# The last rows of each expert's list in one tile of its own size, with the odd quarter of 32 rows computed in column groups of TensorE

## The chip, the core and the metric

The program runs on one core of one Trainium2 chip. Its time is the device time of one execution, in microseconds; of several executions the median is given. A profile is one more execution, recorded by the hardware profiler. In it PE is TensorE (matmuls), PEld its weight loads, DVE is VectorE, ACT is ScalarE, POOL is GpSimd and SP the engine whose queue issues most of the DMA transfers.

## What is computed

One layer over 4096 nodes of 256 features: a graph attention with four heads over a dense 0/1 adjacency matrix, and then a mixture of eight experts of which each node uses two. Cut to what matters:

```python
def gnn(x, adj, W, a1, a2, Wr, br, gamma, beta):
    h = einsum('nd,hdk->hnk', x, W)
    e = leaky_relu(s_row[:, :, None] + s_col[:, None, :], 0.2)
    att = softmax(where(adj > 0, e, -9e15))
    y = elu(att @ h) + x @ Wr + br
    return layernorm(y) * gamma + beta

def ffn(x, Wg, bg, W1, b1, W2, b2):          # 8 experts, top 2
    top_w, top_i = top_k(x @ Wg + bg, 2)
    w_dense = sum(one_hot(top_i) * softmax(top_w)[..., None])
    for e in range(8):
        h = gelu(x @ W1[e] + b1[e])          # 256 -> 1024
        out += w_dense[:, e:e + 1] * (h @ W2[e] + b2[e])

x = x + gnn(layernorm(x), adj, ...)
x = x + ffn(layernorm(x), ...)
```

## The kernel before

**Attention.** The first part, to about 779 us, runs over four passes of 1024 columns. After each pass the 1024 nodes are finished (ELU, residual, layer norms) and routed: their normalised rows are scattered into one list for each expert, in HBM (`lists`, 4608 rows of room each), by indirect DMA from POOL. So the lists are known in steps, after 2048, 3072 and all 4096 nodes.

**Jobs of the experts.** The second part takes rows from the lists in jobs. A job is one expert and a tile of its list. Its rows are brought in, turned so that features lie on the partitions (`turn`), multiplied by W1 (`up`: for each of 8 blocks of 128 hidden features two matmuls into a PSUM tile `ph`, then a Gelu on ScalarE into `hT`), and multiplied by W2 (`down`: for each chunk of 128 rows eight matmuls into `po`). VectorE makes `o` from `po`, each row's share and the scaled second bias, and POOL adds `o` to the rows of the output by an indirect scatter-add. Every scatter-add waits until the one before it has landed. Scores, weights and rows are fp32.

There are 33 jobs. Nine full tiles of 256 rows are planned from the first 2048 nodes (`early`) and eight from 3072 (`mid`). What is left of each list is planned when all nodes are routed, in `plan_rest`: tiles of 256 rows (`rest`, of which 14 are always run), and tiles of 384 rows for lists whose last tile would hold 128 rows or fewer (`broad`, of which two are always run). The two `broad` jobs come right after the full tiles, then the 14 of `rest`. In rows of TensorE's work this is 17 x 256 + 2 x 384 + 14 x 256 = 8704, in 68 chunks. If the lists need more tiles than these, an optional part (`further`) runs them after everything else, behind a test of counters.

**Rooms.** Weights, rows, `xT` and `hT` have two buffers each, `ph` three PSUM banks, `po` two, `o` nine.

**Order.** TensorE's order is fixed by hand (`queue`, L458) until the last two blocks of nodes are routed; they are finished while the first five jobs run (`between`, L1835). After that the scheduler orders by the program's priorities, which gives `ph` of a job, the next tile's transposes, `po` of the job, and so on. SP issues transfers one after another in the order of the loop: for each job `fetch` (L1681) brings b2, w1 and w2, one job ahead; each waits in the queue until its buffer is free. The rows of full tiles come as whole rows (`load_full`, L1857) and are turned by TensorE. Tiles 1 to 15 are loaded ahead of the loop, into 15 buffers, and tile 16 in its third round. The rows of later jobs come as 32-column blocks (`load_blocks_of`, L495) and are turned by VectorE. Both loads wait for the scatters noted so far in `listed`:

```python
        def load_rows_of(t, i, xr):
            rows = t["parts"] * CH
            first = entry(t, 1, i, E * LIST - WT)
            ins = nc.sync.dma_start(
                xr, lists[bass.ds(first, rows), :].rearrange("(c p) d -> p c d", p=CH)
            ).ins
            for i in listed:
                after(ins, i, "rows of the tile")
```

`listed` is emptied when the experts begin (the earlier scatters are long done), and filled again by the routing of the last two blocks: eight scatters each, noted in the fourth and in the fifth round of the loop. After the second block `plan_rest` fills the tables, and POOL writes zeros behind the end of each list (L443), so that a tile may read past it.

Of the kernel before, what the change touches and what calls it, by code (L numbers as in the profile page):

```python
# [18 lines left out]
P = 128  # L19
# [10 lines left out]
CH = P  # L30
TT = 2 * CH
WT = 3 * CH
# [11 lines left out]
def gat_then_moe(  # L44
# [35 lines left out]
    LATE = (2 * N + E * (TT - 1)) // TT - BOTH  # L80
    SURE, SURE_WIDE = 14, 2
# [52 lines left out]
    inside = numbers("inside", [CH, 3], [[CH, 3]], step=1)  # L134
# [82 lines left out]
    def forward(apart, stack):  # L217
# [49 lines left out]
        def tables(tag, width):  # L267

            return {
                "expert": moe_tile(f"expert{tag}", [P, width]),  # L270
                "mark": moe_tile(f"mark{tag}", [P, width]),
                "own": moe_tile(f"own{tag}", [P, width, E]),
                "place": moe_tile(f"place{tag}", [P, width]),
                "rows": moe_tile(f"rows{tag}", [P, width]),
                "float": moe_tile(f"float{tag}", [P, 2, width]),
                "int": moe_tile(f"int{tag}", [P, 2, width], I32),
                "past": moe_tile(f"past{tag}", [P, width, E]),
                "parts": 3 if tag == "w" else 2,
                "upto": moe_tile(f"upto{tag}", [P, E]),
            }  # L280
# [61 lines left out]
        early, mid, rest, broad = tables("e", EARLY), {}, {}, {}  # L342
# [32 lines left out]

        def plan_rest():
# [3 lines left out]
            broad.update(tables("w", E))  # L380
# [7 lines left out]
            tiles = whole("r", left, 0.0)  # L388
            full = whole("h", left, float(CH))
            odd = moe_tile("odd", [P, E])  # L390
            nc.vector.tensor_tensor(odd, tiles, full, OP.subtract)
            nc.vector.tensor_scalar(full, tiles, 2.0, None, op0=OP.is_ge)
            nc.vector.tensor_tensor(odd, odd, full, OP.mult)
            nc.vector.scalar_tensor_tensor(tiles, odd, -2.0, tiles, op0=OP.mult, op1=OP.add)
            plan(rest, LATE, n, tiles, used)
            nc.vector.tensor_tensor(used, used, tiles, OP.add)
            plan(broad, E, n, odd, used)
            counts = moe_tile("counts", [P, 4])
            nc.vector.tensor_copy(counts[:, 0:1], rest["upto"][:, E - 1 :])
            nc.vector.tensor_copy(counts[:, 1:2], broad["upto"][:, E - 1 :])  # L400
            more = moe_tile("more", [P, 3])
            nc.vector.tensor_scalar(more[:, 0:1], counts[:, 0:1], SURE + 0.5, None, op0=OP.is_gt)
            nc.vector.tensor_scalar(
                more[:, 1:2], counts[:, 1:2], SURE_WIDE + 0.5, None, op0=OP.is_gt
            )
            nc.vector.tensor_copy(more[:, 2:3], strayed)
            nc.vector.tensor_reduce(counts[:, 2:3], more, AX.X, OP.max)
            nc.vector.tensor_copy(counts[:, 3:4], strayed)
# [3 lines left out]
            for t, name in (rest, "r"), (broad, "w"):  # L412
                width = t["own"].shape[1]
                spare = moe_tile(f"spare{name}", [CH, width, t["parts"]])
# [71 lines left out]
        def load_rows_of(t, i, xr):  # L486
            rows = t["parts"] * CH
            first = entry(t, 1, i, E * LIST - WT)
            ins = nc.sync.dma_start(
                xr, lists[bass.ds(first, rows), :].rearrange("(c p) d -> p c d", p=CH)  # L490
            ).ins
            for i in listed:
                after(ins, i, "rows of the tile")

        def load_blocks_of(t, i, xb, known):  # L495


            first = entry(t, 1, i, E * LIST - WT)
            rows = lists[bass.ds(first, t["parts"] * CH), :]
            begun = [nc.sync.dma_start(known, rows[:, D:].rearrange("(c p) d -> p c d", p=CH))]  # L500
            for c in range(DC):
                for a in range(P // Q):
                    here = c * P + a * Q
                    begun.append(nc.sync.dma_start(
                        xb[ts(a, Q), c], rows[:, here : here + Q].rearrange("(k p) d -> p k d", p=Q)
                    ))
            for ins in begun:
                for i in listed:
                    after(ins.ins, i, "rows of the tile")
# [1163 lines left out]
        count = kept.tile([P, 4], I32, name="count")  # L1673
# [5 lines left out]
        full_rows = [xr0]  # L1679

        def fetch(t, i):  # L1681

            nch = t["parts"]
# [3 lines left out]
            else:  # L1687
                xr = work.tile([P, DC, t["parts"] * CH // Q, Q], F32, tag="xr", name="xr")
                known = work.tile([CH, t["parts"], RW - D], F32, tag="known", name="known")
# [11 lines left out]
            job = {"t": t, "i": i, "xr": xr, "known": known, "w1": w1, "w2": w2, "nch": nch, "b2b": b2b}  # L1701
            job["last"] = t is rest and i == SURE - 1
# [4 lines left out]
        def prepare(job):  # L1707
# [17 lines left out]
            else:  # L1725
                no = work.tile([CH, nch], F32, tag="no", name="no")
                nc.vector.scalar_tensor_tensor(
                    no, inside[:, :nch], t["rows"][:CH, i : i + 1], t["spare"][:, i, :],
# [15 lines left out]
        def turn(job):  # L1744
            xr, nch = job["xr"], job["nch"]
# [7 lines left out]
            xT = work.tile([P, DC, nch * CH], F32, tag="xT", name="xT")  # L1753
# [10 lines left out]
        def up(job, xT):  # L1764

            nch = job["nch"]
            hT = work.tile([P, FC, nch * CH], F32, tag="hT", name="hT")
            for f in range(FC):
                tag = ("acc00", "acc10", "acc01")[turns[0] % 3]
                ph = ps.tile([P, nch * CH], F32, tag=tag, name="ph")  # L1770
# [15 lines left out]
        def down(job, hT):  # L1786
# [4 lines left out]
            for k in range(nch):  # L1791
                b2s.append(work.tile([CH, D], F32, tag="b2s", name="b2s", bufs=4 if apart else 3))
# [3 lines left out]
            for k in range(nch):  # L1796
                if optional[0]:
                    po = bank([CH, D], "po")
                else:
                    po = ps.tile([CH, D], F32, tag=("acc11", "den")[rounds[0] % 2], name="po")  # L1800
                rounds[0] += 1
                for f in range(FC):
                    order_of(nc.tensor.matmul(  # L1803
                        po, hT[:, f, ts(k, CH)], w2[:, f, :], start=(f == 0), stop=(f == FC - 1)
                    ))
                if k + 1 == nch:
                    yield
# [3 lines left out]
                else:  # L1811
                    o = work.tile([CH, D], F32, tag="o", name="o", bufs=2 * LAG - 3 if apart else 2)
                given_out.append(nc.vector.scalar_tensor_tensor(  # L1813
                    o, po, share[:, k : k + 1], b2s[k], op0=OP.mult, op1=OP.add
# [3 lines left out]
                    bass.IndirectOffsetOnAxis(ap=ids[:, k : k + 1], axis=0), o, None,  # L1818
# [4 lines left out]
                else:  # L1823
                    add()  # L1824

# [24 lines left out]
        todo += [(broad, i) for i in range(SURE_WIDE)] + [(rest, i) for i in range(SURE)]  # L1850
# [6 lines left out]
        def load_full(i):  # L1857
            xr = work.tile([CH, 2, RW], F32, tag="early", name="early", bufs=BOTH - 2)
# [3 lines left out]
        for i in range(1, BOTH - 1):  # L1862
# [7 lines left out]
        for i in range(len(todo)):  # L1870
# [3 lines left out]
            if i == 2:  # L1874
                load_full(BOTH - 1)
# [23 lines left out]
        def further():  # L1899
# [3 lines left out]
            with (  # L1903
# [3 lines left out]
                for k, t, least, top in (0, rest, SURE, LATE), (1, broad, SURE_WIDE, E):  # L1907
                    tiles = held(k, top)
                    with ExitStack() as nest:
                        for i in range(least, top):  # L1910
                            nest.enter_context(tc.If(tiles > i))
                            given_out.clear()
                            job = fetch(t, i)
                            for _ in down(job, up(job, turn(job))):
                                pass
# [5 lines left out]
    with tc.If(held(2, 1) > 0):  # L1921
        further()
        with tc.If(held(3, 1) > 0):
            with ExitStack() as again:
                held, further, rest_of_sums, _ = forward(False, again)
                with tc.If(held(2, 1) > 0):
                    further()
# [35 lines left out]
```

## Time and profile before

| | |
|---|---|
| median of 3 runs | 1286.02 us (1284.5 to 1286.14) |
| the profiled execution, its own time | 1281.97 us |
| its span in the profile | 1280.3 us |
| TensorE busy | 1260.4 us, 98% of the span |
| VectorE busy | 848.7 us, 66% |
| ScalarE busy | 466.8 us, 36% |
| POOL busy | 241.2 us, 19% |
| `w` from HBM, 66 transfers | 1024 KB each |
| chain that ended last | TensorE 92%, VectorE 4% |

The span runs from the first to the last recorded instruction; the execution's own time holds also what lies around it. Busy time of TensorE says that something was in its pipeline, not that it ran at its peak. A matmul of fp32 appears as two instructions, its two passes. In a group, the mean is the latency of one instruction; instructions overlap, so what one costs is the distance between the starts of consecutive ones. The words after an arrow name what ended the idle time ahead of an instruction.

### The profile page before, as it was taken

To read this page: it belongs to the slowest core of one execution; us is meant where nothing else is said; L and a number is where in the kernel's file an instruction comes from. 1 tells how busy PE (TensorE), PEld (TensorE's weight loads), DVE (VectorE), ACT (ScalarE), POOL (GpSimd) and SP (SyncE) were. 2 spreads that over 40 slices of the span, in tenths; PEclk is the share of its full clock that TensorE was granted. 3 is DMA by queue.
4 is the path that set the end of the run, shared out by engine and by line. 5 is a ranking of instruction groups with operands and counts; after the bars stand their busy time and mean duration, and the time that the engine had idled before them with its cause. 6 is when DMAs were issued, how large, how long until landed. Compare 5 with 4: busy or idle time off the path is not lost.

```text
span 1280.3 us, 23272 instructions
## 1 busy us (share of the span) xinstructions
PE 1260.4 (98%) x9102; PEld 698.4 (55%) x9102; DVE 848.7 (66%) x1619; ACT 466.8 (36%) x977; POOL 241.2 (19%) x217
## 2 busy tenths in 40 slices
PE   9999999999999999999999999999999999999997
PEld 5444444332233322322334326878888877888886
DVE  6998887979999999999999995834111111211110
ACT  4322322265432464323644314432333333233232
POOL 4000000001004400006010051244222222122122
PEclk9999999999999999999999999999999999999999
DMA  6334433527433647335563326966866776888882
GB/s 211 114 118 129 152 100 100 189 82 170 154 104 122 206 115 212 103 104 164 128 198 128 120 75 221 284 179 207 260 162 175 198 180 140 201 216 186 209 207 30
DMA packets 144152, 203.36 MB, mean 159 GB/s; under 512 B 49785, under 2 KB 113265, under 8 KB 143649
## 3 DMA queue, kind: packets, MB, share of 16 engines
q1 hardware_dynamic: 122128, 159.16, 41.4%
q0 software_dynamic: 20416, 36.07, 12.8%
q10 hardware_dynamic: 1488, 6.55, 1.4%
q8 instruction: 73, 1.20, 0.4%
q14 instruction: 47, 0.38, 0.1%
HBM read 169.53 MB, written 29.07 MB: 155 GB/s over the span
## 4 chain that ended last, share of the span: by engine, by line
PE 92%; DVE 4%; issue 1%; another core or an unknown queue 1%; DMA 1%; ACT 1%; POOLq 0%; SPq 0%; DVEq 0%; ACTq 0%
PE acc L1112 33%; PE po L1803 18%; PE ph L1773 18%; PE den L1121 16%; PE pr L967 2%; DVE w L1602 2%; PE ph L1015 2%; PE pt L521 1%; PE acc L808 1%; PE ptx L1167 0%; DMA early<-lists 0%; PE pt L694 0%; PE ptr L1405 0%; PE pl L1178 0%
## 5 line engine op out<-in xcount | busy, mean ns | idle before, releaser
L1112 PE MATMUL acc<-w,ha 128*32 128x512 f32 x4096 | 669.9, 593 | 1.3 <-ACT u L1315 0.9
L1602 DVE SCALAR_TENSOR_TENSOR w<-er,eb,am 128x1024 f32<-128x1024 f32 x496 | 606.1, 1275 | 30.4 <-PE den L1121 30.1
L1121 PE MATMUL den<-w,unit 128*2 128x512 f32 x2048 | 466.9, 592 | 0.1
L1112 PEld LDWEIGHTS acc<-w,ha 128*32 128x32 f32 x4096 | 184.5, 110 | 292.8 <-issue 253.8
L1519 ACT ACTIVATE am<-adj 128x1024 bf16<-128x1024 int32 x124 | 130.6, 1054 | 346.4 <-DVE w L1602 208.3
L1773 PE MATMUL ph<-xT,w 128*128 128x256 f32 (+1 forms) x1056 | 243.1, 388 | 3.8 <-issue 3.1
L1803 PE MATMUL po<-w,hT 128*128 128x256 f32 x1088 | 240.2, 379 | 0.0
L1777 ACT ACTIVATE hT<-ph,bias 128x256 f32<-128x256 f32 (+1 forms) x264 | 126.4, 481 | 299.0 <-PE ph L1773 199.9
L1773 PEld LDWEIGHTS ph<-xT,w 128*128 128x128 f32 x1056 | 201.1, 191 | 40.3 <-issue 5.2
L1803 PEld LDWEIGHTS po<-w,hT 128*128 128x128 f32 x1088 | 205.5, 190 | 27.7
L1813 DVE SCALAR_TENSOR_TENSOR o<-po,share,b2s 128x256 f32<-128x256 f32 x66 | 31.9, 483 | 258.9 <-PE po L1803 237.1
L1121 PEld LDWEIGHTS den<-w,unit 128*2 128x2 f32 x2048 | 93.5, 85 | 148.2 <-issue 139.8
L1824 POOL DMA_INDIRECT out<-o,ids x66 | 103.4, 1566 | 338.6 <-DMA out<-o,ids 213.5
L1299 POOL DMA_INDIRECT lists<-xe,at x64 | 88.3, 1380 | 266.6 <-issue 184.3
L525 DVE COPY xT<-pt 128x256 f32<-128x256 f32 x12 | 5.1, 424 | 61.9 <-PE pt L521 61.9
L1795 ACT ACTIVATE b2s<-b2b,share 128x256 f32<-128x256 f32 x68 | 30.8, 503 | 0.0
L967 PE MATMUL pr<-wr,xT 128*128 128x256 f32 x128 | 30.4, 381 | 0.2 <-ACT er L1061 0.2
L1355 POOL DMA_DIRECT2D xf<-in_x x6 | 8.1, 1346 | 103.7 <-ACT xf L1354 103.7
L1035 POOL DMA_DIRECT2D residual<-rb x6 | 4.7, 785 | 121.2 <-DVE rb L982 121.2
L967 PEld LDWEIGHTS pr<-wr,xT 128*128 128x128 f32 x128 | 24.1, 190 | 5.4 <-issue 0.9
L1015 PE MATMUL ph<-wall,xT 128*128 128x264 f32 x96 | 24.6, 399 | 0.0
L1015 PEld LDWEIGHTS ph<-wall,xT 128*128 128x128 f32 x96 | 17.2, 189 | 12.6 <-issue 10.2
(396 smaller groups left out, 653.8 us busy)
## 6 DMA issues: line engine op xcount, KB each, us to landing
w<-in_L_ffn_W SPq DMA_DIRECT2D x66, 1024.0 KB
adj<-in_adj SPq DMA_DIRECT2D x126, 512.0 KB
er<-parts ACTq DMA_DIRECT2D x3, 2048.0 KB
b2b<-in_L_ffn_b SPq DMA_DIRECT2D x33, 128.0 KB
early<-lists SPq DMA_DIRECT2D x16, 260.0 KB
residual<-rb POOLq DMA_DIRECT2D x8, 512.0 KB
rb<-residual SPq DMA_DIRECT2D x8, 512.0 KB
out<-y POOLq DMA_DIRECT2D x8, 512.0 KB
```

Of the source, the lines that this page charges most:

```text
L967: order_of(nc.tensor.matmul(pr[:, k, :], turned[b][:, c, ts(t0 + k, P)], wr[:, c, :], start=(c == 0), stop=(c == DC - 1),))
L1015: order_of(nc.tensor.matmul(phs[t - t0], xT[:, c, ts(t, P)], wall[:, c, :], start=(c == 0), stop=(c == DC - 1),))
L1112: queue(nc.tensor.matmul(acc[half][h // 2][here : here + Q, :], ha[:, j, h * K + g * Q : h * K + (g + 1) * Q], w[half][h], start=(j == 0), ...
L1121: queue(nc.tensor.matmul(den[here : here + HB, :], unit[:, j, h, 1 - half : 1 - half + HB], w[half][h], start=(j == 0 and half == 0), stop ...
L1299: ins = nc.gpsimd.indirect_dma_start(lists, bass.IndirectOffsetOnAxis(ap=at[:, k, t : t + 1], axis=0), xe[:, t, :], None,).ins
L1519: nc.scalar.activation(am, at, AF.Relu, scale=2.0)
L1602: marks["w"] = nc.vector.scalar_tensor_tensor(wh[:, these], er[:, these, h], eb[:, j, h : h + 1], mask[:, these], op0=OP.max, op1=OP.min,).ins
L1773: order_of(nc.tensor.matmul(ph, job["w1"][:, c, ts(f, P)], xT[:, c, :], start=(c == 0), stop=(c == DC - 1),))
L1777: job["gelu"] = nc.scalar.activation(hT[:, f, :], ph, AF.Gelu, bias=job["bias"][:, f : f + 1]).ins
L1803: order_of(nc.tensor.matmul(po, hT[:, f, ts(k, CH)], w2[:, f, :], start=(f == 0), stop=(f == FC - 1)))
L1813: given_out.append(nc.vector.scalar_tensor_tensor(o, po, share[:, k : k + 1], b2s[k], op0=OP.mult, op1=OP.add).ins)
L1824: add()
```

## The change

After the 17 full tiles, each list now ends in one single tile, `final`. `plan_rest` gives a list full `rest` tiles as long as at least 256 rows would still be left, and `plan_final` takes the remainder, up to 511 rows. The eight remainders are sorted by size, and the tile of each rank has a fixed number of rows: 512, 480, 480, 480, 416, 416, 384 and 288 (`FINAL`, in quarters of 32). Two `rest` tiles are always run, after the eight `final` ones. A remainder that is larger than the slot of its rank is completed in the optional part (`plan_over`).

A job may now have up to four chunks, and its last one may be partial. With 96 rows left over it is a chunk of 96, computed first. With 32 (or 64) left, the eight matmuls over the hidden features are spread over four column groups of TensorE, 32 output columns each, into the four quarters of one PSUM tile; VectorE copies this to `pieces`, and one matmul with a matrix of ones and zeros (`joined`) adds the quarters.

In rows this is 17 x 256 + 3456 + 2 x 256 = 8320, in 27 jobs. `hT`, now up to 512 rows wide, has one buffer instead of two. Full tiles have ten row buffers instead of 15: tiles 1 to 10 are loaded ahead of the loop, and tiles 11 to 16 one in each of its rounds 2 to 7, behind the `fetch` of that round. The zero fill behind each list is 512 rows instead of 384.

```diff
 TT = 2 * CH
-WT = 3 * CH
+WT = 4 * CH
+FINAL = (16, 15, 15, 15, 13, 13, 12, 9)
...
-    LATE = (2 * N + E * (TT - 1)) // TT - BOTH
-    SURE, SURE_WIDE = 14, 2
+    LATE = 2 * N // TT - BOTH
+    SURE = 2
+    ROOM = 10
...
+        def plan_final(n):
+
+            t = final
+            wide = [P, E, E]
+            t.update({
+                name: moe_tile(name + "f", shape) for name, shape in (
+                    ("own", wide), ("past", wide), ("expert", [P, E]), ("mark", [P, E]),
+                    ("place", [P, E]), ("rows", [P, E]), ("float", [P, 2, E]),
+                )
+            })
+            t["int"] = moe_tile("intf", [P, 2, E], I32)
+            own, past = t["own"], t["past"]
+            size, key = moe_tile("size", [P, E]), moe_tile("key", [P, E])
+            nc.vector.scalar_tensor_tensor(
+                size, used, -float(TT), n, op0=OP.mult, op1=OP.add
+            )
+            nc.vector.scalar_tensor_tensor(
+                key, size, float(E), order, op0=OP.mult, op1=OP.add
+            )
+            nc.vector.tensor_tensor(
+                past, key.unsqueeze(1).to_broadcast(wide),
+                key.unsqueeze(2).to_broadcast(wide), OP.is_gt,
+            )
+            nc.vector.tensor_reduce(key, past, AX.X, OP.add)
+            nc.vector.tensor_tensor(
+                own, key.unsqueeze(1).to_broadcast(wide),
+                num[:, :E].unsqueeze(2).to_broadcast(wide), OP.is_equal,
+            )
+            for what, into in (order, "mark"), (used, "place"), (size, "rows"):
+                nc.vector.tensor_tensor(past, own, what.unsqueeze(1).to_broadcast(wide), OP.mult)
+                nc.vector.tensor_reduce(t[into], past, AX.X, OP.add)
+            table = t["float"]
+            nc.vector.tensor_scalar(
+                t["expert"], t["mark"], -1.0, float(E), op0=OP.mult, op1=OP.add
+            )
+            nc.vector.tensor_scalar(t["place"], t["place"], float(TT), None, op0=OP.mult)
+            nc.vector.tensor_copy(table[:, 0], t["expert"])
+            nc.vector.scalar_tensor_tensor(
+                table[:, 1], t["expert"], float(LIST), t["place"], op0=OP.mult, op1=OP.add
+            )
+            nc.vector.tensor_copy(t["int"], table)
+
...
+        def plan_over():
+
+            t = over
...
-            tiles = whole("r", left, 0.0)
-            full = whole("h", left, float(CH))
-            odd = moe_tile("odd", [P, E])
-            nc.vector.tensor_tensor(odd, tiles, full, OP.subtract)
-            nc.vector.tensor_scalar(full, tiles, 2.0, None, op0=OP.is_ge)
-            nc.vector.tensor_tensor(odd, odd, full, OP.mult)
-            nc.vector.scalar_tensor_tensor(tiles, odd, -2.0, tiles, op0=OP.mult, op1=OP.add)
+            tiles = whole("r", left, TT - 0.5)
+            nc.vector.tensor_scalar(tiles, tiles, -1.0, 0.0, op0=OP.add, op1=OP.max)
             plan(rest, LATE, n, tiles, used)
             nc.vector.tensor_tensor(used, used, tiles, OP.add)
-            plan(broad, E, n, odd, used)
-            counts = moe_tile("counts", [P, 4])
+            plan_final(n)
...
+        def rows_of_job(t, i):
+            return FINAL[i] * Q if t is final else TT
+
         def load_blocks_of(t, i, xb, known):
 
 
             first = entry(t, 1, i, E * LIST - WT)
-            rows = lists[bass.ds(first, t["parts"] * CH), :]
-            begun = [nc.sync.dma_start(known, rows[:, D:].rearrange("(c p) d -> p c d", p=CH))]
+            n = known.shape[1] * CH
+            begun = [nc.sync.dma_start(
+                known, lists[bass.ds(first, n), D:].rearrange("(c p) d -> p c d", p=CH)
+            )]
+            rows = lists[bass.ds(first, rows_of_job(t, i)), :]
...
+        joined = {}
+        for quads in (1, 2):
+            to = kept.tile([P, quads * Q], F32, name=f"joined{quads}")
+            nc.vector.tensor_reduce(
+                to.rearrange("p (q m) -> p q m", m=Q),
+                ident.rearrange("p (q b m) -> p q m b", q=quads, m=Q), AX.X, OP.add,
+            )
+            joined[quads] = to
...
-            nch = job["nch"]
-            hT = work.tile([P, FC, nch * CH], F32, tag="hT", name="hT")
+            rows = job["rows"]
+            hT = work.tile([P, FC, rows], F32, tag="hT", name="hT", bufs=1)
...
+            def product(k, size):
+
+                po = room()
                 for f in range(FC):
                     order_of(nc.tensor.matmul(
-                        po, hT[:, f, ts(k, CH)], w2[:, f, :], start=(f == 0), stop=(f == FC - 1)
+                        po[:size], hT[:, f, k * CH : k * CH + size], w2[:, f, :],
+                        start=(f == 0), stop=(f == FC - 1),
                     ))
-                if k + 1 == nch:
-                    yield
+                return po
...
+            full, some = divmod(job["rows"], CH)
+            split = some in (Q, 2 * Q)
+            chunks = [(k, CH) for k in range(full)]
+            if split:
+                quads = some // Q
+                groups = FC // (P // Q // quads)
+                po = room()
+                for n in range(groups):
+                    for g in range(P // Q):
+                        q, b = divmod(g, P // Q // quads)
+                        f = b * groups + n
+                        here = full * CH + q * Q
+                        order_of(nc.tensor.matmul(
+                            po[ts(g, Q)], hT[:, f, here : here + Q], w2[:, f, :],
+                            start=(n == 0), stop=(n == groups - 1),
+                        ))
+                pieces = work.tile([P, D], F32, tag="pieces", name="pieces", bufs=1)
+                nc.vector.tensor_copy(pieces, po)
+            elif some:
+                chunks.insert(0, (full, some))
+            for n, (k, size) in enumerate(chunks):
+                po = product(k, size)
+                if n + 1 == len(chunks):
+                    yield
+                give(k, size, po)
+                if split and n == 0:
+                    po = room()
+                    order_of(nc.tensor.matmul(
+                        po[:some], joined[quads], pieces, start=True, stop=True
+                    ))
+                    give(full, some, po)
...
-        todo += [(broad, i) for i in range(SURE_WIDE)] + [(rest, i) for i in range(SURE)]
+        todo += [(final, i) for i in range(E)] + [(rest, i) for i in range(SURE)]
...
-            xr = work.tile([CH, 2, RW], F32, tag="early", name="early", bufs=BOTH - 2)
+            xr = work.tile([CH, 2, RW], F32, tag="early", name="early", bufs=ROOM)
...
-        for i in range(1, BOTH - 1):
+        for i in range(1, ROOM + 1):
...
-            if i == 2:
-                load_full(BOTH - 1)
+            if i >= 2 and len(full_rows) < BOTH:
+                load_full(len(full_rows))
...
+                plan_over()
+                for i in range(E):
+                    with tc.If(held(3 + i, 1) > 0):
+                        extra(over, i)
```

## The prediction

> **What bounds the kernel now.** I read the page from the top: share of each engine, the slices, the chain of waits, the groups; then the timelines of TensorE, of SP's queue and of POOL over the experts' stage. The slices first (a digit is a tenth of busy time, 40 slices of 32 us):
>
> ```profile
> PE   9999999999999999999999999999999999999997
> DVE  6998887979999999999999995834111111211110
> PEclk9999999999999999999999999999999999999999
> DMA  6334433527433647335563326966866776888882
> ```
>
> The experts run from slice 25 on. There VectorE is nearly idle, TensorE full, and the chain of waits from 1000 us to the end is `ph` and `po` alone (96% of it). The groups over the whole span:
>
> ```profile
> L1773 PE MATMUL ph<-xT,w 128*128 128x256 f32 (+1 forms) x1056 | 243.1, 388 | 3.8 <-issue 3.1
> L1803 PE MATMUL po<-w,hT 128*128 128x256 f32 x1088 | 240.2, 379 | 0.0
> ```
>
> Idle time before them is 3.8 us in all, so the time of this stage is the sum of its matmuls. "Mean" is latency; the cost is the distance between starts, read from TensorE's timeline (start, busy, line):
>
> ```profile
> 827.48 0.64 PE L1178 MATMUL pl<-xT,wg 128*32 128x128 f32 x16
> 828.05 7.17 PE L1773 MATMUL ph<-xT,w 128*128 128x256 f32 x32
> ...
> 1036.21 10.48 PE L1773 MATMUL ph<-xT,w 128*128 128x384 f32 x32
> 1046.53 10.52 PE L1803 MATMUL po<-w,hT 128*128 128x256 f32 x48
> 1056.89 10.48 PE L1773 MATMUL ph<-xT,w 128*128 128x384 f32 x32
> ...
> 1264.05 7.07 PE L1803 MATMUL po<-w,hT 128*128 128x256 f32 x32
> ```
>
> Each fp32 matmul is two passes. 48 passes of `po` take 1056.89 - 1046.53 = 10.36 us, 216 ns each; 32 passes of 384 columns take 10.32 us, 323 ns each. The 16 jobs after the full tiles run from 1036.21 to 1264.05 + 6.91 = 1270.96 without a gap: 234.75 us. The span ends 9.3 us later (last scatter-adds).
>
> **What the Trainium skill says.** "TensorE: Matmul & The Clock Gate", Back-to-back issue gap: warm, N/2.4 + 2.5 ns. The trace agrees if a pass counts two cycles a column: 512/2.4 + 2.5 = 215.8, 768/2.4 + 2.5 = 322.5. So a job of R rows costs R x 26.67 ns + 0.08 us for `ph` (32 passes), and 3.45 us for each `po` chunk (16 passes of 256 columns), however few of its 128 rows are used. "TensorEngine Tiling (Array Packing)", Key Properties: column tiles run in parallel, changing the tiling mode drains the array. L1178 above agrees: 16 passes of 128 columns (109 ns each) in four column groups would take 0.44 us; the next mode starts after 0.57, so 0.13 us for a change. "DMA: Bandwidth & Descriptors", Anatomy of one DMA: waits happen on the issuing sequencer before dispatch. The trace shows SP's `w` issues waiting 117.9 us in all for `po`; nothing behind them goes out meanwhile.
>
> **The change part by part.**
>
> *Rows and chunks.* Counting the reference's top-2 experts on its own inputs, the lists after the 17 full tiles hold 492, 359, 462, 470, 392, 476, 277 and 912 rows. The 912 gives two `rest` tiles (SURE = 2) and 400; sorted they are 492, 476, 470, 462, 400, 392, 359, 277 against slots of 512, 480, 480, 480, 416, 416, 384, 288. All fit, the closest by 4 rows, so nothing optional runs. (The same counts give the old plan 2 broad and 14 `rest` jobs, just what the trace shows.)
>
> `ph` in the slots: 13.73 + 3 x 12.88 + 2 x 11.17 + 10.32 + 7.76 = 92.8 us. `po`: 4 + 3 x 4 + 2 x 3 + 3 + 2 = 27 chunks (96 rows cost a whole one) x 3.453 = 93.2. Two `rest` jobs: 2 x 13.81 = 27.6.
>
> *Quarters.* Three slots end in 32 rows: 16 passes in four column groups, 0.86 us if all four overlap, one join of two passes 0.43, three mode changes 0.4. The split reads `hT` 7 early: that Gelu takes about 0.61 us at 416 columns (0.474 at 256, 0.581 at 384) and starts about 0.2 after its matmul, while TensorE arrives 0.5 us after it, so some 0.3 us of wait. About 2.0 each, 6 in all. No trace here has this form with these operands: at best 1.3 each, at worst (no overlap) 3.45 + 0.43 + 0.7 = 4.6, so 4 to 14 us.
>
> Sum: 92.8 + 93.2 + 27.6 + 6 = 219.6 against 234.75: **15.2 us less**.
>
> *One `hT`.* In the changed program's order on TensorE, `po` of a job stays ahead of `ph` of the next, except one block of two matmuls (four passes) slipped ahead of the last chunks of three split jobs. Their Gelu must wait for the old `hT`, but three `ph` banks take further blocks, and after `po` ends the Gelu (0.6 us) is shorter than the next two blocks. Zero; without those banks about 1 us a job.
>
> *Planning.* `plan_final` puts some 40 short VectorE instructions of 0.15 to 0.3 us where about as many of the broad plan go out; the plan ran 862 to 876 us, its tables are first read by SP about 1009. `joined` adds two reduces, about 0.3 us each, near 780 us. Zero for TensorE; both can move the routing of the last rows by half a microsecond.
>
> *Chunk copies and adds.* Scatter-adds stay 68. `pieces` is one 0.45 us VectorE copy under a 3.45 us chunk. Weights: 12 MB fewer, of 66.
>
> *Row loads moved in SP's queue.* This is the part that can cost. Before, all but one row load went out ahead of the loop. With ROOM = 10 the loads of tiles 11 to 16 sit between the weight loads of jobs 3 to 8. Those of tiles 13 and 14 come after the routing of the last two blocks was written down, so they wait for those scatters into `lists`. The one of tile 13 (eight scatters issued 852 to 862) has b2b, w1 and w2 of job 6 behind it; that of tile 14 has those of job 7. Before, on SP and on POOL:
>
> ```profile
> 872.57 0.35 SPq L1693 DMA_DIRECT2D b2b<-in_L_ffn_b  x1
> 873.48 0.37 SPq L514 DMA_DIRECT2D w<-in_L_ffn_W  x1
> 878.34 0.37 SPq L1700 DMA_DIRECT2D w<-in_L_ffn_W  x1
> ```
>
> ```profile
> 881.23 0.97 POOL L1299 DMA_INDIRECT lists<-xe,at  x1 [0.31 <-issue]
> 887.42 0.59 POOL L443 DMA_DIRECT2D lists<-zeros  x1 [5.22 <-DMA lists<-xe,at]
> ```
>
> The last scatter has landed by 887.4. Then SP needs 0.4 + 0.9 + 0.9 us, so w1 of job 7 leaves at 889.6 instead of 873.5, and `ph` of job 7 started at 894.12. One MB at the 363 to 396 GB/s that the busiest stretches show is 2.8 us; [...]beside eight zero fills, now 520 KB instead of 390, it lands between 894 and 899. Against that: w1 and w2 of job 6 also leave later (about 869, due by 878), so POOL's earlier scatter-adds have freer DMA and the scatters could be 2 to 4 us earlier. Stall 0 to 8 us, at the far end with a slower clock after the gap (0.79 granted in 861 to 869, where TensorE had idled 2.6 us). I take 1.
>
> Profiled execution: 1281.97 - 15.2 + 1 = 1267.8. The runs' median lies 4.05 above it; I keep that: 1286.02 - 14.2 = **1271.8 us**.
>
> **The rivals.**
>
> *The moved loads stall TensorE.* As above, 5 to 8 us, perhaps once more at job 6: 1276 to 1281. For it: SP's queue is in order, and the zero fills (4.2 MB) meet w1. Against: everything else at job 7 has slack.
>
> *The scatter-adds become the bound.* They go one after another on POOL:
>
> ```profile
> 1245.88 1.55 POOL L1824 DMA_INDIRECT out<-o,ids  x1 [6.24 <-DMA out<-o,ids]
> 1251.97 1.55 POOL L1824 DMA_INDIRECT out<-o,ids  x1 [4.53 <-DMA out<-o,ids]
> 1256.53 1.55 POOL L1824 DMA_INDIRECT out<-o,ids  x1 [3.01 <-DMA out<-o,ids]
> 1261.06 1.55 POOL L1824 DMA_INDIRECT out<-o,ids  x1 [2.98 <-DMA out<-o,ids]
> ```
>
> From 1085 on every one waits for the one before, 6.9 us apart, as fast as chunks come. If 6.9 is their floor, 34 of them need 234.6 us and the gain is only a longer tail: 1286. It decides above 219.6/34 = 6.5 us. Against: once the weight loads stop, they are 4.5 us apart, and the DMA has a third less to do. Nine `o` tiles buffer them.
>
> *A list overflows.* If one remainder exceeds its slot (4 rows are the closest), the optional part runs after everything: a load of 2.1 MB with nothing to hide it (8 us), 13.8 us of matmuls, its plan and scatter-add (10 us): some +32, so 1304, slower. The old trace, whose counts match, speaks against it. The same holds for "the change doesn't do what it says".
>
> **How the numbers follow.** Forecast 0.62 (1268 to 1276 by the bounds above: a stall of 0 to 4, quarters of 4 to 8); moved loads stall 0.20 (1276 to 1281); better than forecast 0.07 (the waits around 862 and 882 us, 6 us beyond the bare matmuls, shrink as POOL and SP shift); scatter-adds bind 0.05 (1283 to 1287); overflow or another loss 0.06 (above 1289). Two in ten left out: 1267 to 1281; the likeliest's own range is 1268 to 1276. 0.2% is 2.6 us, about what a measurement of this kernel can tell: faster below 1283.4 is 0.62 + 0.20 + 0.07 + 0.01 = 0.90, same 0.04, slower 0.06.
>
> **What would show it.** TensorE's timeline: the part after the last full tile about 219.6 us, `ph` of 512 columns 13.7 us, the 96-row chunk 3.45, each split 1.0 to 1.6 to the next chunk. SP's queue: row loads of tiles 13 and 14 waiting for `lists<-xe,at`, then w1 late; a gap at job 7 is the stall. POOL: scatter-adds under 6.4 us apart. No matmuls of the optional part. Wrong if column groups don't overlap, if gaps appear at each job (one `hT`), or if the tail exceeds 9.3 us.

## The result, and the profile after

The changed kernel takes 1281.84 us in the median of 12 runs (1280.41 to 1282.79), the kernel before beside it 1286.08 us (12 runs, 1281.25 to 1288.17): ratio 0.9971, interval 0.9960 to 0.9983. That is a gain of 0.3%, 4.2 us, where 14.2 were forecast, and the time lies just above the range. The profiled execution took 1281.52 us, its span is 1279.9 us: in the two profiles, kernel before and kernel after end within half a microsecond of each other.

The slices of the changed kernel (40 of 32 us, a digit is a tenth):

```profile
PE   8999999999999999999999999999699999999997
PEclk9999999999999999999999999999799999999999
```

Compare with the rows of before: there TensorE had a 9 in every slice of the experts' stage but the last. Here slice 28 (896 to 928 us) has a 6, and the granted clock falls to 7 in the same slice. The groups say what TensorE waited for; the last number is the wait of that releaser:

```profile
L1848 PE MATMUL ph<-xT,w 128*128 128x256 f32 (+5 forms) x864 | 232.7, 426 | 16.0 <-DMA w<-in_L_ffn_W 14.7
L1882 PE MATMUL po<-w,hT 128*128 128x256 f32 (+1 forms) x1040 | 229.7, 379 | 0.0
```

Before, the idle time ahead of `ph` was 3.8 us in all, most of it with no releaser that the profile names; now it is 16.0, and 14.7 of that is one transfer of weights. TensorE's timeline shows where:

```profile
886.11 7.07 PE L1882 MATMUL po<-w,hT 128*128 128x256 f32 x32
893.02 0.82 PE L586 MATMUL pt<-ident,early 128*128 128x128 f32 x6
908.53 8.83 PE L1848 MATMUL ph<-xT,w 128*128 128x256 f32 x32 [14.69 <-DMA w<-in_L_ffn_W]
917.20 7.07 PE L1882 MATMUL po<-w,hT 128*128 128x256 f32 x32
```

`ph` of job 7 comes 14.69 us late. It also takes 917.20 - 908.53 = 8.67 us from start to start where that of an undisturbed full job takes 6.91. The table of stretches shows why; PEclk is the column after POOL:

```profile
885.00:893.00 8.00, 8.00 (x40) 6.99 (x40) 0.91 (x2) 1.92 (x6) 3.81 (x7) 1.00 0.84 325
893.00:901.00 8.00, 0.84 (x7) 0.58 (x5) 1.48 (x8) 0.37 (x1) 2.17 (x2) 0.83 0.73 231
901.00:909.00 8.00, 0.47 (x1) 0.47 (x2) 0.00 (x0) 0.00 (x0) 1.55 (x1) 0.50 0.80 240
909.00:917.00 8.00, 8.00 (x32) 6.75 (x32) 0.00 (x0) 3.30 (x7) 1.55 (x1) 0.82 1.08 368
```

The clock fell to half while TensorE stood still. In half-microsecond stretches it falls between 898.0 and 898.5 us, over 4 us after TensorE stopped at 893.8, and is full again by 912.0, about 3.4 us into job 7: 1.8 us more. So the stall costs 14.7 + 1.8 = 16.5 us. The Trainium skill says in "TensorE: Matmul & The Clock Gate", Part 1, that after an idle window of about 3.4 us the clock is at half, and that a busy window of the same length brings it back. An estimate from that page, 3.4 us at half speed, is 1.7 us lost; the trace has 1.8. The traces do not bear out the page's length of the idle window: they show the same loss after shorter waits too (second group).

Everything after the full tiles went as forecast. The start of the first slot and TensorE's last jobs:

```profile
1051.72 13.90 PE L1848 MATMUL ph<-xT,w 128*128 128x512 f32 x32
1065.46 13.98 PE L1882 MATMUL po<-w,hT 128*128 128x256 f32 x64
...
1265.16 7.07 PE L1882 MATMUL po<-w,hT 128*128 128x256 f32 x32
```

From 1051.72 to 1265.16 + 6.91 = 1272.07 it is 220.35 us; 219.6 were predicted, 234.75 it was before. No matmul of the optional part runs. The gain of 14.4 us is there. The stall ate it.

### The profile page after: what moved, and what is told of

Same layout as the page of the kernel before. It is cut to its first block, busy times and chain, and to the rows that moved or that the text cites. A ratio compares the mean times of both kernels' runs of the same rounds, so it can differ in the third digit from the quotient of the medians.

```text
span 1279.9 us, 22496 instructions
## 1 busy us (share of the span) xinstructions
PE 1247.8 (97%) x8916; PEld 654.9 (51%) x8916; DVE 842.5 (66%) x1566; ACT 451.4 (35%) x929; POOL 235.0 (18%) x217
## 4 chain that ended last, share of the span: by engine, by line
PE 90%; DVE 4%; issue 2%; DMA 2%; ACT 1%; POOL 1%; POOLq 1%; SPq 0%; DVEq 0%; ACTq 0%
PE acc L1177 33%; PE po L1882 17%; PE den L1186 16%; PE ph L1848 16%; PE pr L1032 2%; DVE w L1667 2%; PE ph L1080 2%; POOL lists L1364 1%; DMA w<-in_L_ffn_W 1%; PE pt L586 0%; PE ptx L1232 0%; DMA early<-lists 0%; PE acc L873 0%; DMA lists<-zeros 0%; PE pt L759 0%
## 5 line engine op out<-in xcount | busy, mean ns | idle before, releaser
L1848 PE MATMUL ph<-xT,w 128*128 128x256 f32 (+5 forms) x864 | 232.7, 426 | 16.0 <-DMA w<-in_L_ffn_W 14.7
L1882 PE MATMUL po<-w,hT 128*128 128x256 f32 (+1 forms) x1040 | 229.7, 379 | 0.0
L1852 ACT ACTIVATE hT<-ph,bias 128x256 f32<-128x256 f32 (+5 forms) x216 | 111.1, 517 | 302.5 <-PE ph L1848 190.4
L1882 PEld LDWEIGHTS po<-w,hT 128*128 128x128 f32 (+1 forms) x1040 | 194.9, 189 | 30.7 <-issue 3.4
L1848 PEld LDWEIGHTS ph<-xT,w 128*128 128x128 f32 x864 | 164.3, 191 | 77.5 <-issue 40.0
L1895 DVE SCALAR_TENSOR_TENSOR o<-po,share,b2s 128x256 f32<-128x256 f32 (+2 forms) x66 | 31.8, 483 | 220.8 <-PE po L1882 185.3
L1364 POOL DMA_INDIRECT lists<-xe,at x64 | 83.6, 1306 | 265.5 <-issue 183.3
L1832 DVE STREAM_TRANSPOSE xT<-xr 128x960 f32<-128x960 f32 (+5 forms) x10 | 10.0, 1005 | 32.1 <-PE ph L1848 31.2
```

Source lines behind the costliest of these rows:

```text
L1364: ins = nc.gpsimd.indirect_dma_start(lists, bass.IndirectOffsetOnAxis(ap=at[:, k, t : t + 1], axis=0), xe[:, t, :], None,).ins
L1848: order_of(nc.tensor.matmul(ph, job["w1"][:, c, ts(f, P)], xT[:, c, :], start=(c == 0), stop=(c == DC - 1),))
L1852: job["gelu"] = nc.scalar.activation(hT[:, f, :], ph, AF.Gelu, bias=job["bias"][:, f : f + 1]).ins
L1882: order_of(nc.tensor.matmul(po[:size], hT[:, f, k * CH : k * CH + size], w2[:, f, :], start=(f == 0), stop=(f == FC - 1),))
L1895: given_out.append(nc.vector.scalar_tensor_tensor(o[:size], po[:size], share[:size, k : k + 1], b2s[k][:size], op0=OP.mult, op1=OP.add,).ins)
```

## Where w1 of job 7 was

The chain of waits, in order of time, through the stall (start, duration, what):

```profile
893.87 5.45 DMA lists<-zeros
899.69 0.38 SPq L548
900.12 0.27 SPq L540
900.64 0.35 SPq L1767
901.03 0.27 SPq L540
901.55 6.94 DMA w<-in_L_ffn_W
```

Read it from the end: w1 of job 7 was 6.94 us on its way, and left only at 901.55. Ahead of it in SP's queue stand b2b (L1767) and a row load (L548); that row load began when the last zero fill of `lists` had landed. SP's queue and SP's waits (total, times, longest) say the same:

```profile
862.92 0.37 SPq L548 DMA_DIRECT2D early<-lists  x1
863.85 0.34 SPq L1767 DMA_DIRECT2D b2b<-in_L_ffn_b  x1
864.75 0.37 SPq L579 DMA_DIRECT2D w<-in_L_ffn_W  x1
865.40 0.37 SPq L1774 DMA_DIRECT2D w<-in_L_ffn_W  x1
899.69 0.38 SPq L548 DMA_DIRECT2D early<-lists  x1
900.64 0.35 SPq L1767 DMA_DIRECT2D b2b<-in_L_ffn_b  x1
901.55 0.37 SPq L579 DMA_DIRECT2D w<-in_L_ffn_W  x1
```

```profile
SPq L548 <- DMA lists<-zeros: 32.8, 1, 32.8
SPq L548 <- DMA lists<-xe,at: 6.4, 1, 6.4
```

SP stood at one row load for 32.8 us and issued nothing. The load is that of tile 14; it is not needed before job 14, 100 us later. What it waited for can be read on POOL:

```profile
881.62 0.97 POOL L1364 DMA_INDIRECT lists<-xe,at  x1 [0.30 <-issue]
885.01 0.58 POOL L502 DMA_DIRECT2D lists<-zeros  x1 [2.42 <-issue]
...
893.87 0.53 POOL L502 DMA_DIRECT2D lists<-zeros  x1 [1.03 <-issue]
```

The prediction let the load wait for the scatters, which end here. But the zero fills behind them also write `lists`, at places known only at run time. In the program they stand ahead of this load: `plan_rest` is called from `between(9)`, in round 4 of the loop, and `load_full(14)` in round 5. So the load waits for the eighth fill as well, issued at 893.87 and landed at 899.3.

Theory: a row load behind the zero fills holds the weights of job 7 in SP's in-order queue. Rivals: the scatters alone hold it long enough; the fills matter as traffic (4.2 MB beside w1) and not as an order; the number of late row loads counts; it takes the rest of the change to make the stall. Three groups of runs followed, on three different chips. The kernel before took from 1273.9 to 1286.1 us in the medians of these groups and the first runs, so each time is compared with the kernel before of its own group.

## First group: which late load does the harm

*ROOM = 15.* All row loads but one go out ahead of the loop, as before.

```diff
-    ROOM = 10
+    ROOM = 15
```

> The changed kernel with ROOM = 15 in place of 10: tiles 1 to 15 are loaded ahead of the loop as in the kernel before, and only that of tile 16 goes out inside it, in round 2. All the rest of the change stays. Theory (a row load that must wait for the zero fills of `lists` holds the weights of job 7 in SP's queue): no gap ahead of `ph` of job 7; the 16.5 us lost there come back, 1281.8 - 16.5 = 1265.3, or 1269.5 if the 4 us that jobs 5 and 6 were shorter go back too. Rival (the queue is not the cause, w1 of job 7 is late because the DMA engines are busy with the larger zero fills): the gap stays, at least 1278.

1259.93 us against 1273.91 for the kernel before: ratio 0.9884 (0.9866 to 0.9902), 14.0 us saved where 14.2 had been forecast for the change. The idle time ahead of `ph` is 0.2 us in all. Undoing this one move brings the whole forecast gain back. The rival of traffic falls: the fills are as large as in the changed kernel. (In the changed kernel's own trace the last of them had landed at 899.3 us, before w1 of job 7 left.)

*ROOM = 13.* Three late loads, all ahead of the fills.

```diff
-    ROOM = 10
+    ROOM = 13
```

> The changed kernel with ROOM = 13: the loads of tiles 14, 15 and 16 go out in rounds 2, 3 and 4, so they stand behind some of the scatters into `lists` but ahead of the zero fills, which are written in round 4 behind them. Theory (zero fills): no gap at job 7, 1265 to 1270. Rival (waiting for the scatters of the last two blocks is already enough to starve TensorE): a gap of 2 to 8 us ahead of job 5, 6 or 7, 1270 to 1278.

1259.23 us, ratio 0.9875 (0.9856 to 0.9895). TensorE's timeline at job 7:

```profile
880.93 7.07 PE L1882 MATMUL po<-w,hT 128*128 128x256 f32 x32
887.84 7.07 PE L1848 MATMUL ph<-xT,w 128*128 128x256 f32 x32
```

No gap. Here SP waited 15.0 us for scatters, in three loads, and lost nothing by it.

*ROOM = 12.* One more, and just this one, tile 16 in round 5, stands behind the fills.

```diff
-    ROOM = 10
+    ROOM = 12
```

> The changed kernel with ROOM = 12: tiles 13 to 16 are loaded in rounds 2 to 5, so just one row load, that of tile 16 in round 5, stands behind the zero fills, with the weights of job 7 behind it. Theory (zero fills): the gap at job 7 is as long as with ROOM = 10, 13 to 16 us, and the time 1279 to 1283. Rival (the number of row loads between the weights counts): four late loads in place of six, the gap falls to about two thirds, 1276 to 1277.

1274.89 us, ratio 1.0001 (0.9991 to 1.0010): 15.7 us above ROOM = 13. The gap is back, at the same job:

```profile
888.38 0.82 PE L586 MATMUL pt<-ident,early 128*128 128x128 f32 x6
901.11 9.48 PE L1848 MATMUL ph<-xT,w 128*128 128x256 f32 x32 [11.92 <-DMA w<-in_L_ffn_W]
```

The gap is a microsecond shorter than expected, but the time is not two thirds of the stall: the number of late loads doesn't count. One load costs all of it.

*Fills later.* ROOM = 10 and all six late loads stay; only the fills are written behind the last of them.

```diff
+        def fill_ends():
+
             zeros = moe_tile("zeros", [CH, WT // CH * RW])
...
+            if i == 8:
+                fill_ends()
             hT = up(job, xT)
```

> The changed kernel with ROOM = 10 and only the zero fills moved: they are written in round 8, behind the last row load, in place of round 4. The load of tile 14 then waits for the scatters of the last block alone, which have landed by about 887; w1 of job 7 leaves at about 889.5 and lands at 894 to 897. Theory (zero fills): the gap shrinks from 14.7 us to between 0 and 4, 1265 to 1270. Rival (scatters alone hold the queue): the gap stays above 8 us, 1274 or more.

1259.43 us, ratio 0.9876 (0.9856 to 0.9895). Two short stalls are left, at jobs 6 and 7 (in this kernel `ph` is L1850):

```profile
875.41 7.15 PE L1850 MATMUL ph<-xT,w 128*128 128x256 f32 x32 [1.72 <-DMA w<-in_L_ffn_W]
...
891.13 7.15 PE L1850 MATMUL ph<-xT,w 128*128 128x256 f32 x32 [1.23 <-DMA w<-in_L_ffn_W]
```

These two are the price of waiting for the scatters: 2.95 us together, inside the 0 to 8 us of the prediction, which took 1. The granted clock stays at 1.00 behind both, and `ph` of job 7 takes 6.99 us. The prediction had the right order of size for the wait that it looked at. It looked at the wrong one.

## Second group: one part alone, and the kernel before again

*The changed kernel and the kernel before, once more.*

> The changed kernel once more, beside the kernel before on another chip. Theory (the change is worth -14.2 and the stall at job 7 +16.5, and the 4 us at jobs 5 and 6 belong to the first chip): 1 to 3 us slower than the kernel before here. Rival (the shorter jobs 5 and 6 come from the change): 3 to 5 us faster, as at first.

> The kernel before once more, for its trace on this chip. Theory (the waits ahead of blocks of `ph` in jobs 5 and 6, 5.7 us together in the first trace, belong to the chip or the execution): from the start of job 5 to that of job 7 here 28.5 us in place of 34.9. Rival (they belong to the program): about 34.9 again.

The changed kernel took 1281.69 us against 1285.32: ratio 0.9982 (0.9969 to 0.9995), 2 to 4 us faster, where the theory had it 1 to 3 us slower. The copy of the kernel before has 1.0005 (0.9991 to 1.0019). In its trace it needed 31.8 us from job 5 to job 7, between the two numbers expected: 28.5 without waits, 34.9 in the first trace. So the waits ahead of jobs 5 and 6 differ from one execution to the next. With ROOM = 13 they were 0.1 us in one trace and 4.2 in another.

A part of these waits is again the clock. In the first trace of the kernel before, TensorE waits 2.25 us in job 5, and right after that the clock is at half; with ROOM = 13 in the third group it waits 2.16 us in job 6, with the same sequel:

```profile
866.00:868.50 2.50, 2.50 (x7) 1.96 (x8) 2.50 (x22) 0.93 (x3) 0.00 (x0) 0.50 0.56 149
883.50:886.50 3.00, 3.00 (x9) 2.37 (x8) 0.00 (x0) 0.95 (x2) 1.15 (x2) 0.50 0.98 313
```

Both times it lasts some 3.4 us, 1.7 us lost. So a wait of little more than 2 us cost nearly twice its length, where the waits of 1.72 and 1.23 us above cost next to nothing. What decides it isn't shown.

In the changed kernel they are partly free. Job 7 can't begin before w1 lands, and a TensorE that is late to job 6 merely waits less at job 7: with 2.2 us of waits in job 6 the gap is 14.69, with 5.0 it is 10.06. That is why the stall of 16.5 us against a saving of 14.4 still left a small gain over a kernel that pays 3 to 6 us there.

*Ten buffers in the kernel before.* Nothing else of the change.

```diff
+    ROOM = 10
...
-            xr = work.tile([CH, 2, RW], F32, tag="early", name="early", bufs=BOTH - 2)
+            xr = work.tile([CH, 2, RW], F32, tag="early", name="early", bufs=ROOM)
...
-        for i in range(1, BOTH - 1):
+        for i in range(1, ROOM + 1):
...
-            if i == 2:
-                load_full(BOTH - 1)
+            if i >= 2 and len(full_rows) < BOTH:
+                load_full(len(full_rows))
```

> The kernel before with one part of the change alone: ten buffers for the row loads, tiles 11 to 16 loaded in rounds 2 to 7. Theory (a row load behind the zero fills holds the weights of job 7): a gap of 12 to 16 us ahead of `ph` of job 7, the time 13 to 17 us above the kernel before. Rival (it needs the larger zero fills or the new plan): within 3 us of the kernel before.

1296.73 us, ratio 1.0104 (1.0068 to 1.0141): 13.4 us slower by the ratio, 11.4 by the medians. SP's waits and TensorE at job 7:

```profile
SPq L490 <- DMA lists<-zeros: 26.2, 1, 26.2
```

```profile
903.89 8.81 PE L1774 MATMUL ph<-xT,w 128*128 128x256 f32 x32 [5.81 <-DMA w<-in_L_ffn_W]
```

The same mechanism without the new slots, the new plan or the larger fills. The gap itself is 5.8 us and not 12 to 16, since TensorE came to it late: jobs 5 and 6 had lost 1.9 and 5.3 us to other waits and the clock. Job 7 starts 121.9 us after job 0, against 115.3 and 112.1 in the two traces of the kernel before and 109.3 where no wait comes in between.

*One `hT` in the kernel before.*

```diff
-            hT = work.tile([P, FC, nch * CH], F32, tag="hT", name="hT")
+            hT = work.tile([P, FC, nch * CH], F32, tag="hT", name="hT", bufs=1)
```

> The kernel before with one `hT` in place of two, and nothing else. The prediction's step says zero: within 1 us of the kernel before, no idle time ahead of `ph` beyond 3.8 us. Rival (Gelu waits for the last chunk of the job before): about 1 us a job, 30 us slower.

1280.68 us, ratio 0.9974 (0.9960 to 0.9989). No loss, as the prediction said; but a gain of 3.3 us by the ratio, which neither expectation had. Its trace shows no waits in jobs 5 and 6 (28.6 us for both). In the two traces the instructions of each engine stand in the same order from job 0 on. What makes these waits come and go is not settled.

## Third group: the queue, the quarters, and the version to keep

*ROOM = 13 beside the changed kernel.*

> The changed kernel with ROOM = 13 once more, on whichever chip this is, beside the changed kernel itself. Theory: no stall at job 7; the part after the full tiles stays at 220 us, so it beats the kernel before by 14 to 20 us (the 14 us of shorter jobs, and whatever waits at jobs 5 and 6 the kernel before has here) and the changed kernel by 14 to 17. Rival (it was the chip): no more than 5 us below the changed kernel.

> The changed kernel, for the comparison with ROOM = 13 on the same chip. Theory (the stall at job 7 ends when the chain of scatters, zero fills, row load and w1 does, whatever TensorE did before): job 7 starts 122 to 128 us after job 0, as in the two traces of it (126.9 and 125.9), and 14 to 17 us above ROOM = 13. Rival: within 5 us of it.

The kernel before took 1282.57 us here. ROOM = 13: 1265.57, ratio 0.9860 (0.9832 to 0.9888), 17 us saved. The changed kernel: 1273.82, ratio 0.9935 (0.9910 to 0.9959). ROOM = 13 is 8.3 us faster, outside both expectations (14 to 17, or no more than 5). The traces account for most of the rest: the changed kernel's job 7 starts 123.4 us after job 0, earlier than in its other traces (126.9 and 125.9), as POOL's first fill was issued 100.0 us after job 0 and not 103.3; this ROOM = 13 had 4.1 us of waits in job 6, and its job 0 began 4.1 us later. The distance from 109.3 to 123.4 and the slower clock still make about 16.

*Late loads on POOL's queue.* ROOM = 10, fills in place, the same waits, another queue.

```diff
-            first = entry(t, 1, i, E * LIST - WT)
-            ins = nc.sync.dma_start(
+            first = entry(t, 1, i, E * LIST - WT, mybir.EngineType.Pool if late else mybir.EngineType.SP)
+            ins = (nc.gpsimd if late else nc.sync).dma_start(
...
-            load_rows_of(*((early, i) if i < EARLY else (mid, i - EARLY)), xr)
+            load_rows_of(*((early, i) if i < EARLY else (mid, i - EARLY)), xr, i > ROOM)
```

> The changed kernel with ROOM = 10, its zero fills where they were, but the six late row loads issued by POOL instead of SP. The load of tile 14 waits as long as before, yet no weights stand behind it. Theory (the harm is the order of SP's queue, not that rows come late: tile 14 is used only by job 14): no gap at job 7, 14 to 17 us below the changed kernel, at most 3 of it lost to scatter-adds held back on POOL. Rival (the load itself, or its data, is what TensorE waits for): the gap stays at 10 us or more.

1262.57 us, ratio 0.9839 (0.9813 to 0.9864): 11.3 us below the changed kernel, less than expected but with no stall. POOL's queue and TensorE:

```profile
900.12 0.53 POOL L502 DMA_DIRECT2D lists<-zeros  x1 [1.16 <-issue]
900.95 1.63 POOL L1907 DMA_INDIRECT out<-o,ids  x1 [0.30 <-issue]
910.68 0.76 POOL L548 DMA_DIRECT2D early<-lists  x1 [8.10 <-PE ph L1848]
```

```profile
884.12 7.07 PE L1882 MATMUL po<-w,hT 128*128 128x256 f32 x32
891.03 7.07 PE L1848 MATMUL ph<-xT,w 128*128 128x256 f32 x32
```

The row load goes out later than ever, at 910.68, 11 us after that of the changed kernel in its first trace, and the idle time ahead of `ph` is 0.2 us in all. (The profile names a matmul as what ended its wait; whether that was so isn't shown.) Neither the load nor its data was what TensorE lacked: it was the weights behind it. The Trainium skill, "DMA: Bandwidth & Descriptors", Issuing engines are not separate DMA queues, says that starting transfers from several engines saves only the time that the sequencer takes to start them, usually small beside the transfer. The transfers here are the same. What the other queue saves is the wait of the load ahead of the weights on SP, 28.0 us in the changed kernel of this group, and that was not small.

*No quarters.* ROOM = 13, and the last 32 rows of three slots as an ordinary chunk.

```diff
-            split = some in (Q, 2 * Q)
+            split = False
```

> ROOM = 13, and one more part undone: the 32 rows at the end of three slots go through TensorE as an ordinary chunk (16 passes over all columns), not in quarters with a join. Theory (from the trace of the changed kernel a split delays the next chunk by 1.3 us and its join takes 0.55): a chunk of 3.45 us in place of 1.85, three times, 4.8 us slower than ROOM = 13. Rival (the mode changes and the early read of `hT` eat the gain): within 2 us of it.

1266.30 us against 1265.57, intervals that overlap: the waits in jobs 5 and 6 are too uneven for the whole time to tell. TensorE's part after the full tiles tells it, since this part is 220.5 us (with the last matmul's busy time) in every trace with quarters. Here it is 225.13: 4.62 us more, 1.54 for each. A chunk of 32 rows costs TensorE as much as one of 128, in this line together with the three others of its job, 14.04 us to the next `ph`:

```profile
1150.00 14.20 PE L1882 MATMUL po<-w,hT 128*32 128x256 f32 x64
1164.04 11.34 PE L1848 MATMUL ph<-xT,w 128*128 128x416 f32 x32
```

and this is a split with its join in the changed kernel:

```profile
1170.62 1.39 PE L1921 MATMUL po<-w,hT 128*32 128x256 f32 x16
1171.93 3.72 PE L1882 MATMUL po<-w,hT 128*128 128x256 f32 x16
1175.58 0.62 PE L1936 MATMUL po<-pieces,joined 128*32 128x256 f32 x2
```

1.31 us to the next chunk, and 0.55 for the join.

## Why the prediction was wrong

The step that failed is "Row loads moved in SP's queue". Its mechanism was right: SP's queue is in order, the loads of tiles 13 and 14 wait for writes into `lists`, the second has the weights of job 7 behind it, and a gap there shows at job 7 with a slower clock. Its size was wrong, 1 us (bounds 0 to 8) against 16.5. The step listed the scatters as what the load waits for and the zero fills only as traffic that slows w1. Every fill is a write into the same tensor, written in the program ahead of the load. With the fills counted, the step would have read: first fill at 887.4 us and some 9 us to issue eight of them (both from the trace before), then, with the times that the trace after shows, about 5 us to land, 2 us to w1 and 7 us for w1, so `ph` at about 910 where it was due at 894. The rival "The moved loads stall TensorE" stopped at 8 us for the same reason, and so the range ended at 1281.

The forecast's other terms, against the profile after:

| term | predicted | measured |
|---|---|---|
| part after the full tiles | 219.6 us | 220.35 us |
| three quarters in it | 6 us | 6.7 us |
| `ph` of 512 columns | 13.7 us | 13.74 us |
| stall at job 7 | 1 us | 16.5 us |
| waits at jobs 5 and 6 | unchanged | 4.1 us less |
| start of job 0 | unchanged | 2.8 us later |
| tail after TensorE | 9.3 us | 7.8 us |

Added to the 1267.8 forecast for the profiled execution: + 15.5 for the stall, - 4.1, + 2.8, + 0.75 for the last part, - 1.5 for the tail, 1281.3; it took 1281.52. Two of these terms belong to the execution and not to the change: job 0 starts anywhere from 777.1 to 783.5 us in the fourteen traces, with the changed kernel near both ends (777.3 and 783.2), and the waits at jobs 5 and 6 differ as shown above. That the changed kernel still came out a little below the kernel before rests, by this sum, mainly on these waits; as far as the prediction goes it is luck.

*Rows and chunks* was right to the passes: 13.74 + 13.81 us for the slot of 512, no optional part. *Quarters* was right: 1.54 us are saved by each; an ordinary chunk costs 3.45 us and its own wait for the last Gelu 0.33 (25.31 us for such a job where its matmuls sum to 24.98), so a split costs 3.45 + 0.33 - 1.54 = 2.2 us where 2.0 was taken. The column groups overlap: 16 passes of 216 ns, 3.45 us one after another, in 1.3 us. "TensorEngine Tiling (Array Packing)" of the Trainium skill, Key Properties, on column tiles in parallel, is borne out for these operands too. *One `hT`*: no loss; alone in the kernel before it even came out 3.3 us faster, through waits that the prediction had put under "better than forecast" and that are not explained. *Planning* and *chunk copies*: no trace of a cost after job 7. (One reading was loose: VectorE is nearly idle only from slice 28 on, while slices 25 to 27 show 8, 3 and 4 tenths. Nothing in the sum used it.)

*The scatter-adds become the bound* did not come true. POOL near the end of the changed kernel:

```profile
1251.57 1.55 POOL L1907 DMA_INDIRECT out<-o,ids  x1 [4.40 <-DMA out<-o,ids]
1256.12 1.55 POOL L1907 DMA_INDIRECT out<-o,ids  x1 [2.99 <-DVE o L1895]
1260.73 1.55 POOL L1907 DMA_INDIRECT out<-o,ids  x1 [3.06 <-DMA out<-o,ids]
```

4.6 us apart, under the 6.5 from which they would bind, and one of them waits for VectorE's `o` and not for the scatter before. The tail became shorter.

*The median* was the second weak spot. The 4.05 us between profile and median of the kernel before were kept; the changed kernel's median lies 0.3 us above its profile, and its first 12 runs lie within 2.4 us where those of the kernel before spread over 6.9. The stall hides the uneven waits ahead of it. Without the stall the forecast would have stood: less its 1 us for the stall it reads 1270.8 us, and ROOM = 13 has 0.9875 and 0.9860 of the kernel before in two groups, which on the forecast's 1286.0 is 1270 and 1268. That is the version to keep: it beats both kernels, and the POOL variant, with 0.9839, is not told apart from it.

## What to carry to other kernels

When a load is moved behind other work in a queue, list every earlier write to the tensor that it reads, in program order and up to the last one, fills and clean-ups included; then the bound of its wait is when the last of them lands, not the one that carries its data. Whatever is needed soon must not stand behind a load that waits for late writes: load early, write later, or give the waiting load another queue. And a stall that is set by a chain off the engine hides the engine's own jitter ahead of it, so its cost is read as the start of the stalled work against an undisturbed run, not as the idle time alone.

## What the runs showed of the hardware

- A gap of 14.7 us costs TensorE another 1.8 us of slower clock (granted 0.50 in 901 to 909 us), one of 11.9 us (ROOM = 12) 2.4: there `ph` takes 9.3 us instead of 6.91. Gaps of 2.25 and 2.16 us were followed by the half clock too, 1.7 us lost; gaps of 1.2 and 1.7 us were not, and cost 0.1 each (`ph` in 6.99 us).
- Eight fills of 520 KB were issued by POOL over 9 us, and the last landed 5.45 us after its issue.
- 1 MB of weights issued together with w2, b2b and a row load took 6.94 us from issue to landing; the prediction's estimate amounts to 4.4 to 9.4 us.
- One program's executions differ by 3 to 4 us in two jobs, 5 and 6, in which TensorE waits for ScalarE and VectorE (31.8 and 34.9 us for the kernel before, 28.6 and 32.7 for ROOM = 13). In the one trace with one `hT` these waits are absent; the cause is open.
